# Last graph layer: one two-bank PSUM tile for a unit's turned blocks, one bank for a row's sums, one bank for the small products

## The chip, the cores and the metric

The program runs on one core of a Trainium2 chip. The metric is the device time of one execution in microseconds (us). Three executions of the kernel before gave a median of 1551.27 us (1541.69 to 1553.98).

A core has these engines: PE (matrix products and transposes, results go to PSUM only), DVE (elementwise work), ACT (activation functions), POOL, and SP, which here issues DMAs. PSUM has eight banks of 128 partitions by 512 float32 values. Both kernels use all eight in this layer.

## The reference, cut to what matters

Four graph layers run one after the other on 4096 nodes with 64 features and one 4096 x 4096 adjacency matrix. Each is followed by a residual and a layer norm. The change touches the fourth, a hyperbolic layer:

```python
deg = jnp.maximum(adj.sum(axis=1, keepdims=True), 1e-08)
w = adj / deg
log_ij = _logmap(x[:, None, :], x[None, :, :], c)
agg = jnp.einsum('ij,ijc->ic', w, log_ij)
transformed = agg @ weight + bias
return _expmap(origin, transformed, c)
```

The distance of nodes i and j is symmetric. The kernel computes a scalar factor f(i, j) for a pair once and uses it twice: times adj(i, j) for the sum of row i, and, turned, times adj(j, i) for the sum of row j.

## The kernel before, in words

The last layer starts at line 1243. Nodes are taken in 8 groups of 512. A tile is a pair of groups (i, j), with j from i on in an order `seq`, so row i of the triangle has 8, 7, ... 1 tiles, 36 in all. A tile is cut into two units of 128 x 1024 (two blocks of 128 nodes by 512), 72 in all. 28 tiles lie off the diagonal, so 56 units have a turned half.

One step of the loop at line 1508 works at several units at once, some steps apart. A unit passes through these instructions:

- `product` (L1327, PE): four instructions into a two-bank tile `v_ps`, of which there are two.
- `square` (L1336, ACT) reads `v_ps`, and `less_one` (L1353, DVE), Ln (L1520) and Exp (L1521, both ACT) follow.
- `opposite` (L1345, PE): two instructions that add to `v_ps`.
- L1545 (DVE) reads `v_ps` for the last time, which frees the tile for the product two units later. L1547 and L1556 (ACT) follow.
- L1530 (DVE) makes the factor `f`, and L1533 (DVE) multiplies the unit's piece of adj(i, j), `at_d`, by it.
- `turn` (L1371, PE): for each of the unit's two blocks of `mirrored`, four transposes of pieces of `f` into one bank of the tag `post`, and then one DVE product (L1373), 128 x 512, from that bank into `at_m`. It comes a step or two after the tile's second `f`. A tile on the diagonal turns only one half, into one bank (L1364, L1366).
- `gather` (L1387 and L1392, PE): sums over nodes. The product with `at_d` goes to the lower 64 partitions of a bank `sums_ps` and gathers through a whole row of tiles. The one with `at_m` goes to the upper 64 partitions of the same bank and lasts for one tile. A tile's upper half is added to `tb` by DVE (L1401 or L1403), and a row's lower half is copied to `tb` by ACT (L1406). A row has a `sums_ps` tile of its own.

When a row's sums are done, `finals` puts its closing steps on a list `seam`, from which each loop step takes one: `first` (L1443 on PE, then L1445 to L1448 on DVE), `second` (L1454 and L1455 on PE, L1459 on ACT, L1460 to L1462 on DVE), and three steps without PE. What is left on the list after the loop runs one after the other. At the head of the layer the list still holds closing steps of layer three (`summed` L1114, `turn_prepared` with the transposes of L212). `right` (L1283 to L1287) makes two operands for a new row through two tiles of `post`.

The order on each engine is not the order of the text. A scheduler goes through the program with an estimate of each instruction's time, gives each engine the earliest instruction of the program that it believes ready, and sets the semaphores. A tile from a pool with n buffers can be written only when the tile n allocations before it (of the same tag) has been read for the last time. Each engine then works through its list in order, and an instruction that waits holds up everything behind it on that engine.

PSUM in this layer: `ps_v3` 2 tiles of two banks, `ps_p3` 2 banks of the tag `post` (turned blocks, `right`, the diagonal's turn, `finals`, the closing steps of layer three), `ps_a3` 2 banks for `sums_ps`.

Of the kernel before, what the change touches and what calls it, by code (L numbers as in the profile page):

```python
# [9 lines left out]
F32 = mybir.dt.float32  # L10
# [4 lines left out]
ALU = mybir.AluOpType  # L15
AX = mybir.AxisListType
PSUM = bass.MemoryType.PSUM
# [43 lines left out]
def gnn4_kernel(  # L61
# [21 lines left out]
    nc = tc.nc  # L83
    P = 128
# [3 lines left out]
    GW = GB * P  # L88
# [35 lines left out]
    ident = const.tile([P, P], F32, name="ident")  # L124
# [77 lines left out]
    def cols(b):  # L202
        return slice(b * P, (b + 1) * P)
# [252 lines left out]
    with tc.tile_pool(name="acc", bufs=1) as acc_p, tc.tile_pool(name="win", bufs=1) as win_p, tc.tile_pool(  # L456
        name="cols0", bufs=4
    ) as cols_p, tc.tile_pool(name="diag0", bufs=2) as diag_p, tc.tile_pool(
        name="ps_t0", bufs=3, space=PSUM
    ) as ps_t, tc.tile_pool(name="ps_a0", bufs=1, space=PSUM) as ps_a, tc.tile_pool(  # L460
        name="ps_p0", bufs=2, space=PSUM
# [112 lines left out]
        for g in range(NG):  # L574
# [3 lines left out]
            for c in reversed(range(NCH)):  # L578
                raw = first_raw.pop() if first_raw else load_raw(g, c)
                at = (diag_p if c == g else cols_p).tile([P, CB, GW], F32, name="at", tag="at")  # L580
                for k in range(CB):
                    jb = c * CB + k
                    tp = ps_t.tile([P, GW], F32, name="tp", tag="tp")
# [466 lines left out]
    for signed in (True, False):  # L1050
        with tc.If(any_negative > 0) if signed else cmp.Else() as block:
            cmp = block
            with tc.tile_pool(name="cols1", bufs=4 if not signed else 2) as cols_p, tc.tile_pool(name="sign1", bufs=1 if signed else 5) as sg, tc.tile_pool(
                name="tail1", bufs=1
            ) as tl, tc.tile_pool(name="ps_a1", bufs=1 if signed else 2, space=PSUM) as ps_a, tc.tile_pool(
                name="ps_p1", bufs=2, space=PSUM
# [80 lines left out]
    with tc.tile_pool(name="mask2", bufs=3) as mk_p, tc.tile_pool(name="wt2", bufs=3) as wt_p, tc.tile_pool(  # L1137
        name="ps_c2", bufs=1, space=PSUM
    ) as ps_c, tc.tile_pool(name="ps_a2", bufs=1, space=PSUM) as ps_a, tc.tile_pool(
        name="ps_p2", bufs=2, space=PSUM  # L1140
# [5 lines left out]
        def gather_two(jb, half, a, wt, acc):  # L1146

            for r in range(2):
                rows = slice(r * HP, (r + 1) * HP)
                in_order(nc.tensor.matmul(  # L1150
                    acc[2 * a + r], lhsT=(sup_two if r == half else over_two)[rows, jb, :],
                    rhs=wt[half][a][rows, :].bitcast(BF16),
                    start=(jb == NB - 1 and half == 1), stop=(jb == 0 and half == 0), skip_group_check=True,
                ))
# [18 lines left out]
        gathers = []  # L1173
        busy = False
        for turn, groups in enumerate(turns_of):
            cnt = [ps_c.tile([P, GW], F32, name=f"cnt_ps{a}") for a in range(2)]
            acc = [ps_a.tile([P, GW], F32, name=f"acc_ps{q}") for q in range(QG)]
# [5 lines left out]
            for h in reversed(range(2 * NB)):  # L1183
                jb, odd = divmod(h, 2)
                c, k = divmod(jb, CB)
# [16 lines left out]
                if odd:  # L1202
                    continue
                two = [
                    lambda half=half, a=a, jb=jb, wt=wt, acc=acc: gather_two(jb, half, a, wt, acc)
                    for half in (1, 0) for a in range(2)
                ]
# [35 lines left out]
    with tc.tile_pool(name="o3", bufs=1) as op, tc.tile_pool(name="cols3", bufs=3) as cols_p, tc.tile_pool(  # L1243
        name="w3", bufs=4
    ) as wp3, tc.tile_pool(name="el3", bufs=3) as el, tc.tile_pool(name="f3", bufs=2) as fp, tc.tile_pool(
        name="r3", bufs=2
    ) as rp, tc.tile_pool(name="ps_v3", bufs=2, space=PSUM) as ps_v, tc.tile_pool(
        name="ps_p3", bufs=2, space=PSUM
    ) as ps_p, tc.tile_pool(name="ps_a3", bufs=2, space=PSUM) as ps_a:
        HB = CB // 2  # L1250

        tb = op.tile([P, N], F32, name="tb")
# [41 lines left out]
        own, mirrored = {}, {}  # L1294
# [19 lines left out]
        rights, sums, fs = {}, {}, {}  # L1314
# [40 lines left out]
        def turn(n):  # L1355

            t, h = n
            i, j = tiles[t]
            work = []
            if i == j:  # L1360
                tp = ps_p.tile([P, GW], F32, name="post", tag="post")
                for k in range(HB):
                    for b in range(HB):
                        nc.tensor.transpose(tp[:, cols(HB * k + b)], fs[t][:, b, cols(HB + k)], ident)  # L1364
                to = own[t][:, HB:CB, 0 : HB * P]
                work.append(lambda: nc.vector.tensor_tensor(to, tp.rearrange("p (k i) -> p k i", k=HB), to, ALU.mult))  # L1366
                return work
            for b in (HB * h, HB * h + 1):
                tp = ps_p.tile([P, GW], F32, name="post", tag="post")
                for k in range(CB):  # L1370
                    nc.tensor.transpose(tp[:, cols(k)], fs[t][:, k, cols(b)], ident)  # L1371
                to = mirrored[t][:, b, :]
                work.append(lambda to=to, tp=tp: nc.vector.tensor_tensor(to, tp, to, ALU.mult))  # L1373
            return work

        def gather(t, h, tm):
# [131 lines left out]
        while n < NU + 2 or turns or gathers:  # L1508
            if n % 2:
                load_own((n + 1) // 2)  # L1510
                load_mirrored((n - 1) // 2)
            after = gather(*gathers.pop(n)) if n in gathers else []
            turned = [w for what in turns.pop(n, []) for w in turn(what)]
            if n < NU:
                if n % 2 == 0:
# [8 lines left out]
            if n >= 2 and n - 2 < NU:  # L1524
                m = n - 2
                t, h = divmod(m, 2)
# [17 lines left out]
            if n < NU:  # L1544
                nc.vector.scalar_tensor_tensor(rt, vs[n][:, :, cs], V_FLOOR, rt, ALU.max, ALU.add)  # L1545
                product(n + 2)
                nc.scalar.activation(w, w, AF.Exp, bias=half_shift[:, 1:2], scale=-0.5)  # L1547
            late = turn(late_turns.pop(n)) if n in late_turns else []
            for work in after:
                work()  # L1550
# [59 lines left out]
```

## Time and profile before

| | |
|---|---|
| median of three executions | 1551.27 us (1541.69 to 1553.98) |
| the profiled execution's own time | 1546.41 us |
| its span in the trace | 1544.3 us |
| PE busy over the span | 1410.2 us (91%) |
| DVE busy over the span | 1066.9 us (69%) |
| ACT busy over the span | 761.4 us (49%) |
| first `right` of the last layer | at 1071.6 us |
| first transposes of the first off-diagonal tile | at 1103.7 us |
| `at_m` products (L1373) | 112, 75.3 us busy |
| transposes for them (L1371) | 448, 67.4 us busy |

The shares of the whole span mix four layers. The last one alone, cut near the ends of its rows (a cut is where ACT copies a row's sums, rounded), is as follows.

| stretch (us) | length | PE busy | DVE busy | ACT busy |
|---|---|---|---|---|
| 1074 to 1125 | 51 | 43.6 | 46.5 | 44.5 |
| 1125 to 1198 | 73 | 62.6 | 69.5 | 55.2 |
| 1198 to 1279 | 81 | 75.5 | 79.4 | 76.6 |
| 1279 to 1353 | 74 | 67.9 | 68.0 | 65.9 |
| 1353 to 1413 | 60 | 54.3 | 57.0 | 56.3 |
| 1413 to 1462 | 49 | 45.1 | 45.1 | 45.0 |
| 1462 to 1498 | 36 | 33.6 | 33.8 | 33.8 |
| 1498 to 1523 | 25 | 21.8 | 24.5 | 17.0 |
| 1523 to the end | 21.3 | 5.6 | 11.3 | 10.7 |

Busy time is the time in which an engine had an instruction under way, with overlaps counted once. In a line of the timeline, the first number is the start and the second the duration, both in us; what stands in brackets is the engine's idle time before it and who ended it.

### The profile page before, as it was taken

How to read it: one execution, taken by the hardware profiler on the slowest of the kernel's cores; microseconds unless marked ns; L12 is line 12 of the kernel's file. 1: busy time of each engine (PE TensorE's matmuls, PEld its weight loads, DVE VectorE, ACT ScalarE, POOL GpSimd, SP SyncE). 2: the span in 40 equal slices, each digit the busy share in tenths (PEclk: the TensorE clock that was granted, in tenths of full speed). 3: DMA queues.
4: the chain of work that ended last, by engine and by line, in shares of the span. 5: the costliest groups of instructions: out<-in, count | busy, mean ns of one | idle time of the engine just before them, and what ended most of it. 6: DMA issues, size and time to landing. Idle time of an engine off the chain costs nothing.

```text
span 1544.3 us, 19446 instructions
## 1 busy us (share of the span) xinstructions
PE 1410.2 (91%) x7054; PEld 644.7 (42%) x7054; DVE 1066.9 (69%) x2123; ACT 761.4 (49%) x1265; POOL 123.8 (8%) x194
## 2 busy tenths in 40 slices
PE   5999999999999969889899999998888999899995
PEld 4555655554443323334343333333334444344343
DVE  5899989883000663667666422556999999999997
ACT  3544434441000110222222476654877999899995
POOL 3011000000000001222222200000000000000000
PEclk9999999999999998999999999999999999999997
DMA  9999999996787987888888655553224453445430
GB/s 295 412 404 411 411 410 397 382 358 242 245 287 261 389 342 271 280 309 305 296 309 296 207 177 183 164 165 131 88 109 164 162 195 136 167 156 193 149 113 11
DMA packets 103359, 385.38 MB, mean 250 GB/s; under 512 B 16340, under 2 KB 17368, under 8 KB 71256
## 3 DMA queue, kind: packets, MB, share of 16 engines
q1 hardware_dynamic: 84256, 296.78, 53.9%
q0 software_dynamic: 15616, 85.73, 13.6%
q10 hardware_dynamic: 3384, 1.56, 0.4%
q8 instruction: 57, 0.93, 0.2%
q14 instruction: 46, 0.38, 0.1%
HBM read 297.26 MB, written 85.20 MB: 248 GB/s over the span
## 4 chain that ended last, share of the span: by engine, by line
PE 32%; DVE 18%; ACT 6%; issue 2%; DMA 2%; SPq 0%; ACTq 0%; DVEq 0%
PE v_ps L1327 5%; PE a_ps L997 4%; PE sums_ps L1387 4%; PE cnt_ps L1192 4%; PE acc_ps L1150 4%; DVE rt L1545 3%; DVE at_m L1373 3%; PE p_ps L980 2%; DVE f L1530 2%; DVE at_d L1533 2%; ACT wt L1197 2%; PE post L779 1%; DMA at<-adj_t 1%; PE p_ps L988 1%; DVE w L1353 1%
## 5 line engine op out<-in xcount | busy, mean ns | idle before, releaser
L592 ACT COPY at<-tp 128x512 f32<-128x512 f32 x256 | 132.5, 598 | 137.2 <-issue 96.0
L1327 PE MATMUL v_ps<-rv,tr_a 128*128 128x512 f32 (+1 forms) x288 | 141.5, 616 | 31.7 <-DVE rt L1545 30.3
L1197 ACT ACTIVATE wt<-cnt_ps 128x512 uint16<-128x512 f32 x208 | 115.4, 594 | 72.1 <-PE cnt_ps L1192 70.3
L585 PE MATMUL tp<-ident,raw 128*128 128x128 f32 x1024 | 133.4, 284 | 16.2 <-DMA raw<-in_adj_dram 12.0
L618 DVE TENSOR_REDUCE dpart<-raw 128x4 f32<-128x2048 f32 x64 | 145.4, 2272 | 0.4 <-DMA raw<-in_adj_dram 0.3
L620 DVE TENSOR_REDUCE lows<-raw 128x1 f32<-128x2048 f32 x64 | 145.4, 2271 | 0.0
L1387 PE MATMUL sums_ps<-at_d,nat_c 128*64 128x512 f32 x288 | 139.8, 606 | 1.4 <-DVE at_d L1533 1.0
L585 PEld LDWEIGHTS tp<-ident,raw 128*128 128x128 f32 x1024 | 116.6, 145 | 55.3 <-issue 34.1
L997 PE MATMUL a_ps<-at,nat_a 128*64 128x512 f32 x512 | 126.9, 624 | 2.9 <-DVE at L963 2.9
L447 DVE TENSOR_SCALAR pos<-at 128x2048 fp8e4<-128x2048 f32 x72 | 87.1, 1224 | 58.1 <-DMA at<-adj_t 49.3
L1392 PE MATMUL sums_ps<-at_m,nat_c 128*64 128x512 f32 x224 | 108.6, 607 | 0.0
L492 PE MATMUL w_ps<-at,cheb_n 128*128 128x512 f32 x224 | 101.1, 595 | 0.0
L492 PE MATMUL pass<-at,cheb_n 128*128 128x512 f32 x224 | 99.9, 604 | 0.7 <-DVE cheb_n L643 0.7
L1556 ACT ACTIVATE rt<-rt,one_col 128x1024 f32<-128x1024 f32 x72 | 78.7, 1095 | 22.5 <-DVE rt L1545 22.0
L1327 PEld LDWEIGHTS v_ps<-rv,tr_a 128*128 128x128 f32 x288 | 52.8, 199 | 82.7 <-DVE rt L1545 39.5
L1545 DVE SCALAR_TENSOR_TENSOR rt<-v_ps,rt 128x1024 f32<-128x1024 f32 x72 | 83.2, 1156 | 3.8 <-ACT rt L1521 3.6
L1192 PE MATMUL cnt_ps<-m,follow 128*64 128x512 fp8e4 x480 | 81.1, 391 | 4.7 <-ACT wt L1197 2.3
L1533 DVE TENSOR_TENSOR at_d<-at_d,f 128x1024 f32<-128x1024 f32 x72 | 83.2, 1156 | 0.1
L1530 DVE SCALAR_TENSOR_TENSOR f<-rt,w 128x1024 f32<-128x1024 f32 x72 | 82.9, 1158 | 0.5 <-ACT rt L1556 0.4
L1373 DVE TENSOR_TENSOR at_m<-post,at_m 128x512 f32<-128x512 f32 x112 | 75.3, 683 | 9.3 <-PE post L1371 8.6
L1336 ACT ACTIVATE w<-v_ps,one_col 128x1024 f32<-128x1024 f32 x72 | 75.7, 1053 | 11.3 <-PE v_ps L1327 10.9
L1547 ACT ACTIVATE w<-w,half_shift 128x1024 f32<-128x1024 f32 x72 | 78.7, 1094 | 0.9
(365 smaller groups left out, 2267.3 us busy)
## 6 DMA issues: line engine op xcount, KB each, us to landing
at<-adj_t SPq DMA_DIRECT2D x122, 1024.0 KB, 6.1
raw<-in_adj_dram SPq DMA_DIRECT2D x64, 1024.0 KB, 13.7
adj_t<-at POOLq DMA_DIRECT2D x64, 1024.0 KB, 8.2
at_d<-adj_t SPq DMA_DIRECT2D x36, 1024.0 KB, 4.8
at_m<-adj_t SPq DMA_DIRECT2D x28, 1024.0 KB, 6.8
mask_t<-pos POOLq DMA_DIRECT2D x64, 256.0 KB, 5.9
m<-mask_t SPq DMA_DIRECT2D x120, 128.0 KB, 2.8
m<-mask_t SPq DMA_DIRECT2D x60, 256.0 KB, 3.9
```

Of the source, the lines that this page charges most:

```text
L492: in_order(nc.tensor.matmul(ps, lhsT=cheb_n[:, jb, k : k + 2, :], rhs=rhs, start=first, stop=last))
L585: in_order(nc.tensor.transpose(tp[:, cols(b)], raw[:, b, cols(k)], ident))
L592: nc.scalar.copy(at[:, k, :], tp)
L618: in_order(nc.vector.tensor_reduce(dpart[:, g, c, :], raw, AX.X, ALU.add))
L620: in_order(nc.vector.tensor_reduce(lows[:, n : n + 1], raw.rearrange("p b j -> p (b j)"), AX.X, ALU.min))
L997: in_order(nc.tensor.matmul(ps[q * F : (q + 1) * F, :], lhsT=nat_a[:, c * CB + k, 0:F], rhs=parts[q if signed else 0][:, k, :], start=(c = ...
L1192: in_order(nc.tensor.matmul(cnt[a][r * HP : (r + 1) * HP, :], lhsT=follow, rhs=chunks[c][odd][2 * a + r][:, k, :], start=(h == 2 * NB - 1) ...
L1197: in_order(nc.scalar.activation(wt[odd][a], cnt[a], AF.Relu, scale=-128.0))
L1327: nc.tensor.matmul(vs[n][:, k, cs], lhsT=tr_a[:, cols(jb)], rhs=rights[i][0][:, cs], start=True, stop=True)
L1373: work.append(lambda to=to, tp=tp: nc.vector.tensor_tensor(to, tp, to, ALU.mult))
L1387: in_order(nc.tensor.matmul(bank[0:F, :], lhsT=nat_c[:, j * CB + k, :], rhs=own[t][:, k, :], start=(i == j and k == 0), stop=(j == seq[-1] ...
L1545: nc.vector.scalar_tensor_tensor(rt, vs[n][:, :, cs], V_FLOOR, rt, ALU.max, ALU.add)
```

## The change

`ps_p3` and `ps_a3` go from two buffers to one. A unit's eight transposes go into one tile of two banks with a tag of its own (`two`, one buffer), and one DVE product of 128 x 1024 takes the place of two of 128 x 512. All other users of `post` share one bank, and all rows share one bank for `sums_ps`. The eight banks are then 4 for `v_ps`, 1 for `post`, 2 for `two` and 1 for `sums_ps`.

```diff
-        name="ps_p3", bufs=2, space=PSUM
-    ) as ps_p, tc.tile_pool(name="ps_a3", bufs=2, space=PSUM) as ps_a:
+        name="ps_p3", bufs=1, space=PSUM
+    ) as ps_p, tc.tile_pool(name="ps_a3", bufs=1, space=PSUM) as ps_a:
...
-            for b in (HB * h, HB * h + 1):
-                tp = ps_p.tile([P, GW], F32, name="post", tag="post")
+            tp = ps_p.tile([P, HB, GW], F32, name="two")
+            for b in range(HB):
                 for k in range(CB):
-                    nc.tensor.transpose(tp[:, cols(k)], fs[t][:, k, cols(b)], ident)
-                to = mirrored[t][:, b, :]
-                work.append(lambda to=to, tp=tp: nc.vector.tensor_tensor(to, tp, to, ALU.mult))
+                    nc.tensor.transpose(tp[:, b, cols(k)], fs[t][:, k, cols(HB * h + b)], ident)
+            to = mirrored[t][:, HB * h : HB * h + HB, :]
+            work.append(lambda: nc.vector.tensor_tensor(to, tp, to, ALU.mult))
             return work
```

## The prediction

> **What bounds the kernel now.** I first read the page's shares, then the busy time by stretch, because the page mixes four layers. The stretch from the first steady steps of the last layer to its last row (columns: length, then busy us of PE, PE's weight loads, DVE, ACT, POOL):
>
> ```profile
> 1098.00:1515.00 417.00, 380.03 (x1572) 166.71 (x1570) 394.42 (x654) 374.52 (x491) 0.00 (x0) 0.99 0.40 148
> ```
>
> DVE is busy for 394.4 of 417 us (94.6%), PE for 380.0 (91%), ACT for 374.5 (90%). DVE is nearest to the bound, but PE is only 14 us behind it and ACT 20. Then the waits in nearly the same stretch (sum, times, longest, us):
>
> ```profile
> PE v_ps L1327 <- DVE rt L1545: 24.2, 31, 2.6
> ACT rt L1556 <- DVE rt L1545: 22.0, 25, 2.5
> DVE at_m L1373 <- PE post L1371: 8.6, 11, 2.2
> PE post L1371 <- DVE at_m L1373: 6.4, 13, 1.3
> ```
>
> PE and ACT mostly wait for DVE (24.2 and 22.0), which agrees with DVE as the bound. The last two rows are the subject of the change: DVE stood for turned blocks, and PE for a free `post` bank. One unit on DVE, from the timeline:
>
> ```profile
> 1256.79 0.69 DVE L1353 TENSOR_SCALAR w<-w 128x1024 f32<-128x1024 f32 x1
> 1257.40 1.22 DVE L1530 SCALAR_TENSOR_TENSOR f<-rt,w 128x1024 f32<-128x1024 f32 x1
> 1258.65 0.69 DVE L1373 TENSOR_TENSOR at_m<-post,at_m 128x512 f32<-128x512 f32 x1
> 1259.26 1.22 DVE L1533 TENSOR_TENSOR at_d<-at_d,f 128x1024 f32<-128x1024 f32 x1
> 1260.53 0.69 DVE L1373 TENSOR_TENSOR at_m<-post,at_m 128x512 f32<-128x512 f32 x1
> 1261.14 1.22 DVE L1545 SCALAR_TENSOR_TENSOR rt<-v_ps,rt 128x1024 f32<-128x1024 f32 x1
> 1262.27 0.68 DVE L1353 TENSOR_SCALAR w<-w 128x1024 f32<-128x1024 f32 x1
> ```
>
> The next starts come before the recorded ends: a 512-wide product is followed after 0.61 us (recorded 0.69), a 1024-wide one after 1.13 (1261.14 to 1262.27; recorded 1.22). The unit takes 5.48 us on DVE. The durations by shape:
>
> ```profile
> L1545 DVE SCALAR_TENSOR_TENSOR rt<-v_ps,rt 128x1024 f32<-128x1024 f32 x64 | 77.8, 1216 | 3.8 <-ACT rt L1521 3.6
> L1373 DVE TENSOR_TENSOR at_m<-post,at_m 128x512 f32<-128x512 f32 x112 | 75.3, 683 | 9.3 <-PE post L1371 8.6
> ```
>
> L1545 reads a two-bank PSUM tile and a tensor in SBUF, as the new product will, so 1216 ns is the new product's price.
>
> **What the Trainium skill says.** "Perfetto Trace Analysis", section Optimizing Scalar/DVE Operations, puts DVE's access overhead per instruction at about 125 ns on PSUM, half of what is recorded overlapping with the next instruction; it adds that larger operations help a saturated engine. The trace gives 2 x 683 - 1216 = 150 ns by recorded durations and 2 x 0.61 - 1.13 = 0.09 us by starts: the same order, on both sides of the page's figure. The same page, section Identifying Performance Opportunities, says that a repeated gap on the engine that should be saturated can mean too few PSUM buffers; here that is 8.6 us of DVE in 417. "PSUM — Partial Sum Buffer", section PSUM bank collisions raise a hardware error, asks for guards by bank, so a DVE read of a bank and the next PE write to it must take turns; the 6.4 us above are such turns.
>
> **The change part by part.**
>
> *One product for two.* 56 units lose one DVE instruction each: 56 x 0.09 = 5.0 us by starts, 56 x 0.150 = 8.4 by records. I take 0.11 each, 6.2 us, and of that nine tenths, since DVE is busy 94.6% and PE and ACT have little more room: -5.5 (ends 0 and -8.4).
>
> *The transposes' bank.* Count on PE is unchanged (448). A unit's eight now wait for the one product of the unit before. In the unit above the product would stand where the first `at_m` does, 1258.65 to about 1259.8, and PE reaches its transposes at 1260.3 to 1260.8, behind the sums and L1345. Half a microsecond or more is left, and PE idles 0.47 us before the next L1327 at 1262.41 anyway. That cover hides it; without the cover it costs PE whatever the product is late. Before, the second bank came free only at 1261.2, so half of the 6.4 us of PE waits should go. PE is not the bound: 0.
>
> *Less company in `post`.* The turned blocks no longer share banks with `right`, `finals` and the diagonal's turn. Near 1300 to 1307 both banks were held by `right`, whose copies ACT made at 1302.26 and 1302.83, and DVE then waited 1.74 us for transposes. I let six tenths of the 8.6 us go, -5, and charge the other waits for eight transposes in place of four: eight take 1.09 us at 1306.78, so 0.5 more for about 3 of them, +1.5. Sum about -3.5 (ends -8.6, all gone, and +6, eleven waits each 0.55 longer).
>
> *One bank for sums.* A new row's first sums now wait for ACT's copy of the old row. At the second row's end:
>
> ```profile
> 1278.16 0.69 DVE L1403 TENSOR_TENSOR tb<-sums_ps,tb 64x512 f32<-64x512 f32 x1
> 1278.18 1.98 PE L1327 MATMUL v_ps<-rv,tr_a 128*128 128x512 f32 x4
> 1279.22 0.56 ACT L1406 COPY tb<-sums_ps 64x512 f32<-64x512 f32 x1
> ...
> 1280.09 0.64 PE L1387 MATMUL sums_ps<-at_d,nat_c 128*64 128x512 f32 x1
> ```
>
> The copy ends at 1279.78, 0.31 us ahead of the next sums; at the other six row ends it is 0.32 to 1.15. Product L1327 on PE hides it. Behind the waiting sums stand L1345 and the transposes, and for those wait L1545 and `at_m`. Price 0; without that cover at most one ACT instruction (1.1 us) at 7 row ends, +8.
>
> *One bank for small products.* Inside the rows, `right`'s second product waits for ACT's copy of the first (about 0.6 us, 8 times), and at a row's start L1443 waits for L1366, which came at 1204.23, two microseconds after L1443 began at 1202.23. PE idled 1.13 us before 1204.37 and 0.47 on other steps, so most is covered; I put +1 (ends 0 and +7).
>
> *The tail.* Here nothing covers it. The last two rows close one after the other:
>
> ```profile
> 1519.19 1.08 PE L1443 MATMUL post<-spread,tb 128*128 128x65 f32 x8 [0.44 <-DVE th L1482]
> ...
> 1523.12 0.16 DVE L1447 SCALAR_TENSOR_TENSOR al<-al,post 128x4 f32<-128x4 f32 x1
> ...
> 1523.89 1.06 PE L1443 MATMUL post<-spread,tb 128*128 128x65 f32 x8
> ...
> 1525.23 0.41 DVE L1460 TENSOR_TENSOR agg<-post,al 128x256 f32<-128x256 f32 x1
> ...
> 1525.70 0.69 PE L1454 MATMUL post<-spread_w,tb 128*128 128x64 f32 x2 [0.75 <-DVE agg L1460]
> ```
>
> With two banks, row 7's `second` began at 1522.06 beside its `first`, which DVE read until 1523.28, and row 8's `first` ran while `second` held the other bank. With one, row 7's `second` begins 1.2 us later, and behind its L1460 row 8's `first` comes whole: 1.06 on PE, then L1445 to L1447 (1526.67 to 1527.74 before, 1.07), and only then L1454. Sum 1.2 + 1.06 + 1.07 and a few handovers: 3.3 to 4.5, taken as +4.
>
> *Sum:* -5.5 - 3.5 + 0 + 1 + 4 = -4, against the profiled execution's span of 1544.3 and its own 1546.41, that is 1540.3 and 1542.4. That execution lies 4.86 under the median shown; I put the same 4 on the median: 1551.27 - 4 = 1547.3. What is late next in the stage is PE, whose own instructions come to about 5.4 us a unit (1267.61 to 1272.98 without a wait, 5.37).
>
> **The rivals.**
>
> *The shared banks were the real loss* (0.12). If all 8.6 us of DVE's waits go, the DVE saving is whole (8.4) and the smaller waits around them shrink by a further 7 of the 22.6 us in which DVE idled, the stage gains 24 and the tail returns 4: 1531. For it: the stretch 1279 to 1353, with 6 us idle on DVE, has such waits. Against: PE has 37 us of room in 417 and ACT 42, in small pieces.
>
> *DVE time saved is not time saved* (0.25). From 1413 to 1462 PE, DVE and ACT are busy 45.1, 45.1 and 45.0 of 49 us. If the three take turns as the limit everywhere, the stage gives 1 or 2 us and the tail costs 4: 1554.
>
> *The other side, slower* (0.08): the single `two` tile makes PE wait. Place: between L1345 and L1327. It decides when the product ends later than about 1261 in the unit above, that is, when the scheduler puts it behind L1545. It then ends 1262.27 + 1.13 = 1263.4, and the transposes start 2.6 us late, 2.1 beyond the idle 0.47. In one unit of four that is 14 x 2.1 = +29, with the -4 about 1576. For it: the product cannot start until all eight transposes are there, so it falls back in the order more easily. Against: L1545 stands later in the program than the product, and the margins above.
>
> That the merged product costs twice as much across two banks is excluded by L1545's 1216 ns.
>
> **How the numbers follow.** Forecast 0.55 (1541 to 1553, its own range: the ends of its terms partly cancel), rivals 0.12, 0.25 and 0.08. About 1% is what a measurement of this kernel can tell from no change: faster is under 1535.8, slower above 1566.8. The first rival lies under that, the last above it, the rest between: 0.12, 0.80, 0.08. For 8 in 10 the range takes the forecast and the null case, plus the part of the first rival that falls short of its full size: 1536 to 1558.
>
> **What would show it.** Right: 56 `at_m` products of about 1216 ns; DVE busy in the stretch some 5 to 8 us less; DVE's wait on L1371 below 5 us; PE's waits on `at_m` not above 6; L1406 ended before the next L1387; the time from the last sums to the end about 4 longer. Wrong: PE waits on `at_m` of tens of us, `at_m` behind L1545 on DVE, sums that wait for L1406, or a stage shortened by more than 15.

## The result and the profile after

The kernel after takes 1556.4 us (median of 11, 1549.16 to 1559.62), the kernel before 1548.62 (median of 11 measured beside it, 1541.69 to 1553.98). The ratio is 1.0052, with a 95% interval of 1.0034 to 1.0071: slower by some 8 us. The number lies inside the predicted range, but the predicted sign was wrong.

The profiled execution of after took 1558.9 us. Its page begins:

```profile
span 1557.1 us, 19410 instructions
...
PE 1418.1 (91%) x7054; PEld 649.7 (42%) x7054; DVE 1064.8 (68%) x2067; ACT 759.8 (49%) x1265; POOL 123.9 (8%) x194
```

PE is busy for 8 us more than before, DVE for 2 less. The first row below is the stretch of the prediction; the second runs from the layer's first L1327 to the last row's copy L1406, which I call the body; the third is a piece of the layer's start. The columns are those of the prediction; the last three numbers are PE's granted clock, the DMA share and GB/s:

```profile
1098.00:1515.00 417.00, 380.94 (x1563) 166.66 (x1563) 390.08 (x597) 374.73 (x479) 0.00 (x0) 0.98 0.40 148
1080.19:1530.42 450.23, 407.95 (x1649) 179.00 (x1648) 419.65 (x685) 392.24 (x515) 0.00 (x0) 0.97 0.39 143
1075.00:1085.00 10.00, 8.35 (x16) 3.80 (x16) 6.24 (x38) 2.76 (x7) 0.00 (x0) 0.50 1.01 423
```

The same body in the kernel before:

```profile
1074.16:1522.91 448.75, 404.40 (x1656) 178.04 (x1656) 423.58 (x745) 394.05 (x517) 0.00 (x0) 0.98 0.39 147
```

A fixed stretch of time holds another piece of the work when a layer begins later, so I compare bodies. DVE is busy for 3.9 us less, and yet the body is 1.5 us longer. The 12.8 us between the two spans split into four (layer three's sums end with the copies L1215):

| part (us) | before | after | difference |
|---|---|---|---|
| up to the first copy L1215 of layer three's last sums (unchanged code) | 1067.23 | 1069.87 | +2.64 |
| from there to the first L1327 | 6.93 | 10.32 | +3.39 |
| body | 448.75 | 450.23 | +1.48 |
| tail: last row's copy L1406 to the end | 21.39 | 26.68 | +5.29 |

The first part is this one execution's own. The second is its own by half. The layer's start, first before, then after:

```profile
1069.77 2.00 PE L1114 MATMUL post<-wd,sums 128*128 128x64 f32 x16 [2.36 <-DVE sums L1215]
1071.61 1.84 PE L1283 MATMUL post<-tr_a,to_right 128*66 128x512 f32 x2
1073.37 0.58 PE L1286 MATMUL post<-sp_two,to_other 128*2 128x512 bf16 x1
```

```profile
1072.41 3.68 PE L1114 MATMUL post<-wd,sums 128*128 128x64 f32 x16 [2.36 <-DVE sums L1215]
1077.02 1.94 PE L1283 MATMUL post<-tr_a,to_right 128*66 128x512 f32 x2 [0.94 <-DVE ln_st L275]
1079.68 0.58 PE L1286 MATMUL post<-sp_two,to_other 128*2 128x512 bf16 x1 [0.71 <-ACT rv L1284]
```

The sixteen L1114 took 3.68 us in after and 2.00 before. PE's granted clock was 0.50 from 1072 to 1077 in after, and 1.00 before, from 1069.7 to 1071.7. These 1.7 us are not the change's: number 2, whose code is that of before here, has them too. The other 1.7 us are the change's. With one small bank, `right`'s first product stands 0.94 us, until DVE has read the bank of L1114 (L1120, ended at 1076.88; the trace names the instruction behind it), and its second 0.71, until ACT has copied the first. Six of the kernels below with one small bank and L1114 at 2.00 us (numbers 1, 3, 5, 6, 10 and 12) take 8.65 us from L1215 to the first L1327; the three with two or three banks and the same L1114 (before, numbers 4 and 11) take 6.75 to 6.93. Start (+1.7), body and tail together give +8.5, which is close to the +7.8 between the medians. Some of the waits from 1100 to 1515 in after (sum, times, longest, us):

```profile
ACT w L1336 <- PE v_ps L1327: 15.0, 20, 2.1
PE v_ps L1327 <- DVE rt L1545: 14.5, 21, 2.7
PE two L1371 <- DVE at_m L1373: 9.2, 11, 1.5
DVE w L1353 <- ACT w L1336: 6.1, 7, 1.6
DVE agg L1460 <- ACT v L1459: 4.6, 5, 1.7
DVE at_m L1373 <- PE two L1371: 4.5, 8, 1.1
```

DVE's own wait for turned blocks has fallen from 8.6 to 4.5 and PE's wait for `rt` from 24.2 to 14.5. But PE now waits longer for the turned tile (6.4 to 9.2), ACT waits longer for the product (6.8 to 15.0), and DVE waits for ACT's square (0.8 to 6.1). At five row ends DVE also stands before L1460 of `second`, for ACT's L1459 (0.2 to 4.6). The groups by shape show the new product at the price taken for it:

```profile
L1545 DVE SCALAR_TENSOR_TENSOR rt<-v_ps,rt 128x1024 f32<-128x1024 f32 x64 | 78.0, 1219 | 4.3 <-ACT rt L1521 3.0 <-PE v_ps L1345 1.1
L1373 DVE TENSOR_TENSOR at_m<-two,at_m 128x1024 f32<-128x1024 f32 x56 | 68.3, 1220 | 5.5 <-PE two L1371 5.0
```

The timeline of after at a place where two turned units follow one another, and in the tail:

```profile
1343.50 0.98 PE L1371 MATMUL two<-ident,f 128*128 128x128 f32 x7
...
1344.53 1.23 DVE L1373 TENSOR_TENSOR at_m<-two,at_m 128x1024 f32<-128x1024 f32 x1 [0.50 <-PE two L1371]
1345.66 1.22 DVE L1545 SCALAR_TENSOR_TENSOR rt<-v_ps,rt 128x1024 f32<-128x1024 f32 x1
...
1345.80 1.09 PE L1371 MATMUL two<-ident,f 128*128 128x128 f32 x8 [1.10 <-DVE at_m L1373]
...
1522.37 0.64 PE L1387 MATMUL sums_ps<-at_d,nat_c 128*64 128x512 f32 x1 [1.18 <-ACT tb L1406]
...
1526.69 1.10 PE L1443 MATMUL post<-spread,tb 128*128 128x65 f32 x8
...
1530.63 0.16 DVE L1447 SCALAR_TENSOR_TENSOR al<-al,post 128x4 f32<-128x4 f32 x1
...
1530.93 0.41 PE L1454 MATMUL post<-spread_w,tb 128*128 128x64 f32 x2 [1.28 <-DVE ln_ve L246]
...
1533.90 0.43 DVE L1460 TENSOR_TENSOR agg<-post,al 128x256 f32<-128x256 f32 x1 [1.34 <-ACT v L1459]
1534.38 1.97 PE L1443 MATMUL post<-spread,tb 128*128 128x65 f32 x8 [1.48 <-DVE agg L1460]
...
1537.60 0.66 PE L1454 MATMUL post<-spread_w,tb 128*128 128x64 f32 x2 [1.25 <-DVE nv L1470]
```

Two things are to be seen. At 1344 the one tile makes turns strict: transposes, product, transposes. The second eight cannot start before the product ends at 1345.76, and PE stands for 1.10 us although the factors were there. In the tail the four steps stand in one chain through the one bank: row 7's `first` at 1526.69, its `second` only after L1447, row 8's `first` only after L1460, and row 8's `second` only after that row's L1447.

### The profile page after: what moved, and what is told of

It reads as the page before. It is cut to its first block, busy times and chain, and to the rows that moved or that the text cites. A ratio compares the mean times of both kernels' runs of the same rounds, so it can differ in the third digit from the quotient of the medians.

```text
span 1557.1 us, 19410 instructions
## 1 busy us (share of the span) xinstructions
PE 1418.1 (91%) x7054; PEld 649.7 (42%) x7054; DVE 1064.8 (68%) x2067; ACT 759.8 (49%) x1265; POOL 123.9 (8%) x194
## 4 chain that ended last, share of the span: by engine, by line
PE 63%; DVE 19%; ACT 6%; issue 6%; DMA 4%; ACTq 1%; SPq 1%; POOL 1%; DVEq 0%; POOLq 0%
PE tp L585 7%; PE pass L492 6%; PE w_ps L492 6%; PE v_ps L1327 5%; PE a_ps L997 4%; PE sums_ps L1387 4%; PE cnt_ps L1192 4%; PE acc_ps L1150 4%; PE pass L485 3%; PE h_ps L485 3%; DVE rt L1545 3%; DVE at_m L1373 2%; PE post L506 2%; PE p_ps L980 2%; DVE f L1530 2%
## 5 line engine op out<-in xcount | busy, mean ns | idle before, releaser
L1327 PE MATMUL v_ps<-rv,tr_a 128*128 128x512 f32 (+1 forms) x288 | 144.0, 624 | 18.8 <-DVE rt L1545 18.3
L997 PE MATMUL a_ps<-at,nat_a 128*64 128x512 f32 x512 | 123.7, 611 | 2.9 <-DVE at L963 2.9
L1556 ACT ACTIVATE rt<-rt,one_col 128x1024 f32<-128x1024 f32 x72 | 78.7, 1095 | 18.6 <-DVE rt L1545 18.1
L1545 DVE SCALAR_TENSOR_TENSOR rt<-v_ps,rt 128x1024 f32<-128x1024 f32 x72 | 83.4, 1159 | 4.3 <-ACT rt L1521 3.0
L1327 PEld LDWEIGHTS v_ps<-rv,tr_a 128*128 128x128 f32 x288 | 53.2, 202 | 76.9 <-issue 41.9
L1521 ACT ACTIVATE rt<-w,half_shift 128x1024 f32<-128x1024 f32 x72 | 78.5, 1094 | 0.6
```

What stands on the lines that cost most here:

```text
L997: in_order(nc.tensor.matmul(ps[q * F : (q + 1) * F, :], lhsT=nat_a[:, c * CB + k, 0:F], rhs=parts[q if signed else 0][:, k, :], start=(c = ...
L1327: nc.tensor.matmul(vs[n][:, k, cs], lhsT=tr_a[:, cols(jb)], rhs=rights[i][0][:, cs], start=True, stop=True)
```

## The experiments

The theories at the start: the tail is the loss, and the rows gain nothing because what DVE saves comes back as waits for the one tile; or the rows lose because `right`, `finals` and the diagonal's turn take turns in one small bank; or the single sums bank costs. The banks are those of after unless an edit says otherwise. "Rows" are the times between copies L1406 (seven intervals).

**1. The tail alone.** The last two rows' `second` writes to the turned tile, idle by then.

```diff
-                o = ps_p.tile([P, GB, 2, F], F32, name="post", tag="post")
+                if g in seq[-2:]:
+                    o = ps_p.tile([P, HB, GW], F32, name="two")[:, 0, :].rearrange("p (b t f) -> p b t f", b=GB, t=2)
+                else:
+                    o = ps_p.tile([P, GB, 2, F], F32, name="post", tag="post")
```

> The changed kernel, with one difference: the second step of the last two rows takes its PSUM from the turned blocks' two-bank tile, which has no other use by then. Theory (the one small bank makes the two last rows close in single file): the stretch from the last copy of sums to the end falls from 26.7 us back to 21 to 22.5, and the time falls by 4 to 5.5 us, to 1551 to 1552.5. Rival (the loss is in the rows, the longer tail is an effect of the clock there): the stretch stays at 25 to 27 and the time at 1555 to 1557.

1551.83 us, ratio to before 1.0015 (1.0002 to 1.0028), 4.6 less than after. Its tail in the timeline (L1457 is the old L1454):

```profile
1524.82 1.11 PE L1443 MATMUL post<-spread,tb 128*128 128x65 f32 x8
...
1527.71 0.43 PE L1457 MATMUL two<-spread_w,tb 128*128 128x64 f32 x2
...
1528.76 0.16 DVE L1447 SCALAR_TENSOR_TENSOR al<-al,post 128x4 f32<-128x4 f32 x1
...
1531.18 1.45 PE L1443 MATMUL post<-spread,tb 128*128 128x65 f32 x8 [1.47 <-ACT tb L1406]
...
1532.42 0.63 PE L1457 MATMUL two<-spread_w,tb 128*128 128x64 f32 x2
```

Row 7's `second` now runs ahead of its L1447, and row 8's two steps stand close together. The tail falls from 26.68 to 20.15. Rows stay as in after (326.81 against 324.78; six of the seven agree within 0.02 us, the last is 2.0 longer because the last copy now comes later). So the tail's part of the loss is shown.

**2. One bank for sums alone**, in the kernel before.

```diff
-    ) as ps_p, tc.tile_pool(name="ps_a3", bufs=2, space=PSUM) as ps_a:
+    ) as ps_p, tc.tile_pool(name="ps_a3", bufs=1, space=PSUM) as ps_a:
```

> The kernel before with one bank for the rows' sums and nothing else changed (one PSUM bank stays unused). Theory (the copy of a row's sums is hidden): 1548 to 1550, at most one of seven row ends with a wait of a microsecond. Rival (one bank for the sums is what costs): 1552 to 1556, with waits of the first sums of a row for the copy at several row ends.

1549.2 us, ratio 0.9997 (0.9982 to 1.0013). The rows take 324.36 us, against 324.35. The bank costs nothing.

**3. The new division of the banks without the merged product:** two products of 128 x 512, each block in a bank of its own (`ps_t` is a pool of two banks).

```diff
-            tp = ps_p.tile([P, HB, GW], F32, name="two")
-            for b in range(HB):
+            for b in (HB * h, HB * h + 1):
+                tp = ps_t.tile([P, GW], F32, name="two")
...
-            to = mirrored[t][:, HB * h : HB * h + HB, :]
-            work.append(lambda: nc.vector.tensor_tensor(to, tp, to, ALU.mult))
+                to = mirrored[t][:, b, :]
+                work.append(lambda to=to, tp=tp: nc.vector.tensor_tensor(to, tp, to, ALU.mult))
```

> The changed kernel's banks (one for small products, one for sums, two for turned blocks alone) with the old two products of 128x512 per unit. It tells the merging from the banks. Theory (the merged product gains about 5 us in the rows, the banks lose): slower than the changed kernel, 1558 to 1563. Rival (the merged product with its single two-bank tile holds the rows up): faster than the changed kernel, 1549 to 1554.

1558.94 us, ratio 1.0068 (1.0051 to 1.0085). The body takes 448.92 us, between before (448.75) and after (450.23), and the tail 29.61. As the tails differ by 2.9 us from after's, this pair does not price the merging cleanly; number 12 does. DVE's wait for turned blocks falls from 8.6 to 4.2 us, but at five row ends DVE stands 1.6 us each before L1462 (the old L1460), 7.9 in all, against 0.2 before.

**4. Shared banks:** the kernel before with the freed sums bank given to `post`.

```diff
-        name="ps_p3", bufs=2, space=PSUM
-    ) as ps_p, tc.tile_pool(name="ps_a3", bufs=2, space=PSUM) as ps_a:
+        name="ps_p3", bufs=3, space=PSUM
+    ) as ps_p, tc.tile_pool(name="ps_a3", bufs=1, space=PSUM) as ps_a:
```

> The kernel before with one bank for sums and three shared banks for all transposes and small products, two products per unit. Theory (sharing banks with the small products cost DVE waits; a third bank removes them, and the tail keeps two banks): 1543 to 1547. Rival (DVE, PE and ACT take turns as the limit, so fewer waits for banks give nothing): 1547 to 1551.

1540.67 us, ratio 0.9929 (0.9899 to 0.9958): faster than both kernels. Body and waits from its profile:

```profile
1079.15:1523.17 444.02, 402.80 (x1640) 178.89 (x1664) 422.58 (x748) 392.87 (x521) 0.00 (x0) 0.98 0.40 149
```

```profile
PE v_ps L1327 <- DVE rt L1545: 20.4, 25, 2.6
...
DVE at_m L1373 <- PE post L1371: 4.5, 5, 1.8
...
PE post L1371 <- DVE at_m L1373: 3.3, 7, 1.1
```

DVE is as busy as before (422.6 against 423.6), with all 112 products, but DVE's and PE's waits for each other over turned blocks fall together: 8.6 to 4.5 and 6.4 to 3.3. DVE's wait before L1460 is 1.4. The body is 4.7 us shorter. The tail, 19.33, is 2.1 shorter than before; row 8's `first` and `second` find free banks one behind the other:

```profile
1523.80 1.10 PE L1443 MATMUL post<-spread,tb 128*128 128x65 f32 x8 [1.47 <-ACT tb L1406]
1524.74 0.39 PE L1454 MATMUL post<-spread_w,tb 128*128 128x64 f32 x2
```

Numbers 3 and 4 have the same eight banks and the same instructions and stand 18 us apart; they differ in whether three banks are shared or tied to uses (2 + 1). Of that, 15.2 lie behind the first L1327 (10.3 in the tail and 4.9 in the body, but the last row is 3.2 us shorter in number 3, which moves the cut between the two) and 1.8 at the layer's start.

**5. `right` made later**, four steps ahead and not six, on top of number 1. If `right` in the one small bank holds up the rows, it should then meet `finals` less.

```diff
-            if n + 6 < NU and tiles[(n + 6) // 2][0] not in rights:
-                i = tiles[(n + 6) // 2][0]
+            if n + 4 < NU and tiles[(n + 4) // 2][0] not in rights:
+                i = tiles[(n + 4) // 2][0]
```

> The changed kernel with the tail's second step in the two-bank tile, and the operands of a new row made four loop steps ahead in place of six, after the old row's second step has left the small bank. Theory (in the rows the small products stand in each other's way in their one bank): the rows that the changed kernel made longer, the fourth (62.0 us) and the sixth (39.5), come back to 59 to 60 and 35 to 37, and the time falls from 1551.8 to 1545 to 1549. Rival (those rows are long because the merged product makes the order on the engines worse, not because of the small bank): rows four and six stay within 1 us of 62.0 and 39.5, the time at 1550 to 1553.

1557.41 us, ratio 1.0061 (1.0037 to 1.0085), so 5.6 slower than number 1. The sixth row came back from 39.54 to 36.13, but the second, fourth and fifth grew (80.00 to 85.05, 61.99 to 63.45, 46.55 to 51.35). The theory of `right` explains one row and not the sum. It is not refuted either: number 8 shows that the later `right` costs 4.4 us where three banks are shared, so this edit can bring a loss of its own; but numbers 12 and 6, where the same step costs nothing (1551.66 and 1549.15), have one small bank too.

**6. Two products, tail freed, lead of four:** number 3 with the same tail edit (`second` of the last two rows from `ps_t`) and the edit of number 5.

> As the one before, but with two products of 128x512 per unit from two banks of their own: the two kernels differ in the merging alone. Theory (merging saves DVE time, but DVE, PE and ACT take turns as the limit, so little of it is saved time): within 3 us of the kernel with the merged product. Rival (merging saves what DVE saves, 4 to 8 us, once the small bank is out of the way): 4 to 8 us slower than it.

1549.15 us, ratio 1.0004 (0.9992 to 1.0017). With the later `right` the merged form (number 5) is 8.3 us slower than the two products.

**7. `second` of all rows in the turned tile:** the edit of number 1 without its condition.

> The changed kernel with the second step of all rows, not of the last two alone, in the turned blocks' tile: one kind of small product moves from the small bank to the other one. Theory (a bank tied to one use waits while the other is free; sharing is what the old kernel had right): rows four and six shorter than 62.0 and 39.5 by 1 to 3 us each, time 1547 to 1551. Rival (turned blocks then wait for the second step, which ACT and DVE read late): rows 1 to 3 us longer, time 1553 to 1560.

1552.55 us, ratio 1.0025 (1.0012 to 1.0038). Rows four and six shrink against number 1 (61.99 to 58.13, 39.54 to 37.74), row two grows (80.00 to 87.28); the sum is 1.0 longer. Freeing the small bank everywhere gains nothing either: DVE no longer stands before L1460 (4.6 us in number 1), but it waits longer for the sums (L1403, 1.3 to 6.3 us).

**8. Number 4 with the lead of four.**

> Control for the lead of four steps: the kernel with three shared banks and one bank for sums, with the operands of a row made four steps ahead. Theory (the lead matters only where the small bank is single): within 2 us of 1540.7. Rival (the shorter lead is better or worse by itself): differs by over 3 us.

1545.1 us, ratio 0.9965 (0.995 to 0.998), 4.4 slower than number 4 (the intervals overlap slightly); rows 324.17 against 319.55. A change of two steps in the program's text moves the rows by as much as the banks do.

**9. Merged product with shared tiles:** number 1 with the turned blocks and the last `second` steps in a third tile of `v_ps`.

```diff
-    ) as rp, tc.tile_pool(name="ps_v3", bufs=2, space=PSUM) as ps_v, tc.tile_pool(
+    ) as rp, tc.tile_pool(name="ps_v3", bufs=3, space=PSUM) as ps_v, tc.tile_pool(
...
-            tp = ps_p.tile([P, HB, GW], F32, name="two")
+            tp = ps_v.tile([P, HB, GW], F32, name="two", tag="v_ps")
```

> Merged products whose two-bank tile is not tied to the turned blocks: three two-bank tiles shared by v_ps and the turned blocks, one bank for small products, one for sums, the tail's second step in a shared tile. Theory (banks tied to one use are what the merged product loses by): rows shorter than the 324.8 us of the changed kernel by 4 to 8, time 1544 to 1549. Rival (the turned blocks take tiles from the products of v_ps, which PE then cannot start in time): rows longer by 5 to 20, time 1556 to 1572.

1550.64 us, ratio 1.0019 (0.9998 to 1.004). PE's wait moves to the distance product:

```profile
PE v_ps L1327 <- DVE at_m L1373: 32.0, 29, 2.8
```

Tiles of one tag go round in order, so L1327 gets the tile that the last merged product still reads. Sharing is not good by itself; here it ties the main product to the turned one.

**10. Two products from the one two-bank tile.** All else is as in after.

```diff
-            to = mirrored[t][:, HB * h : HB * h + HB, :]
-            work.append(lambda: nc.vector.tensor_tensor(to, tp, to, ALU.mult))
+            for b in range(HB):
+                to = mirrored[t][:, HB * h + b, :]
+                work.append(lambda b=b, to=to: nc.vector.tensor_tensor(to, tp[:, b, :], to, ALU.mult))
```

> The changed kernel with two products of 128x512 read out of the one two-bank tile, so that the first need not wait for all eight transposes, while both banks still come free together. Theory (little of DVE's time is saved time, and the tile held as one costs PE): rows within 3 us of the changed kernel's 324.8, time 1554 to 1560. Rival (the wait for all eight transposes is what eats the gain): rows 4 us or more shorter, time 1549 to 1552.

1563.06 us, ratio 1.0081 (1.0049 to 1.0112), 6.7 slower than after, with intervals that overlap. The traces give 6.0 for body and tail, but 4.5 of it is the tail, where neither kernel has a turned product; the body is 1.5 longer, and the rows are level (324.23 against 324.78). So that merging is right with the one tile is not shown. `PE two <- DVE at_m` is 13.2 us here: two smaller products do not shorten PE's wait as long as the tile is one.

**11. What a microsecond of DVE is worth:** before with one of a unit's two mirrored products left out.

```diff
-                work.append(lambda to=to, tp=tp: nc.vector.tensor_tensor(to, tp, to, ALU.mult))
+                if b == HB * h:
+                    work.append(lambda to=to, tp=tp: nc.vector.tensor_tensor(to, tp, to, ALU.mult))
```

> The kernel before with one of a unit's two products of a turned block left out (the transposes stay), so the sums of mirrored blocks are not the reference's. It takes 56 products of 0.61 us by starts, 34 us of DVE time, away and measures how much of DVE's time is time of the kernel. Theory (DVE, PE and ACT take turns as the limit): 8 to 18 us faster, a quarter to a half of 34. Rival (DVE is the bound, as the prediction took it, nine tenths): 27 to 34 us faster.

1526.07 us, ratio 0.984 (0.9802 to 0.9878), 22.5 less than before. Its body:

```profile
1076.31:1506.47 430.16, 400.73 (x1664) 179.01 (x1664) 394.00 (x693) 391.53 (x518) 0.00 (x0) 0.98 0.41 154
```

DVE's busy time falls by 29.6 us in the body and the body by 18.6: 0.63 of it. On the medians, 22.5 of 29.6 is 0.76, with an interval (18.9 to 30.7 us) that does not exclude nine tenths. DVE is the main bound, but with PE at 400.7 and ACT at 391.5 of 430 us over a third of what it saves in the body is lost. The edit also frees one of a unit's two banks without a read, so the 0.63 is not the worth of DVE's time alone.

**12. The pair of number 1 without the merging:** number 3 with the tail edit only.

> Two products of 128x512 from two banks of their own and the tail's second step in one of these, with the old lead of six steps: it differs from the changed kernel with the mended tail (1551.83) in the merging alone, the third such pair. Theory (the merging's effect has no steady sign; the order the scheduler lays down decides): the tail 19 to 21, the time 1546 to 1554. Rival (merging saves the DVE time that it takes away, two thirds of 4 to 8 us): 1554.5 to 1557. Rival (merging loses, as with the lead of four): below 1547.

1551.66 us, ratio 1.0017 (1.0001 to 1.0033), against 1551.83 for number 1. The two differ in the merging alone (one product and one tile for two), and no difference shows; the intervals are 2 to 2.5 us to either side. In the traces body and tail together are 470.5 us here and 472.3 in number 1. Some of the waits from 1100 to 1515, first of number 12 (lines shifted by two), then of number 1:

```profile
PE v_ps L1329 <- DVE rt L1550: 16.6, 25, 2.1
...
ACT w L1338 <- PE v_ps L1329: 9.8, 12, 1.9
...
DVE agg L1465 <- ACT v L1464: 7.9, 5, 1.6
...
DVE at_m L1375 <- PE two L1373: 4.2, 5, 1.5
...
PE two L1373 <- DVE at_m L1375: 1.7, 6, 0.3
```

```profile
ACT w L1336 <- PE v_ps L1327: 15.3, 19, 2.2
...
PE v_ps L1327 <- DVE rt L1548: 13.6, 20, 2.9
PE two L1371 <- DVE at_m L1373: 11.6, 11, 2.2
DVE w L1353 <- ACT w L1336: 7.1, 7, 1.6
...
DVE agg L1463 <- ACT v L1462: 4.6, 5, 1.7
DVE at_m L1373 <- PE two L1371: 4.5, 8, 1.1
```

With the same two banks, the merged form makes PE wait 11.6 us for the turned tile in place of 1.7. ACT waits 5.5 more for the distance product, and DVE 5.1 more for ACT's square (7.1 against 2.0). In number 12 DVE's largest wait in these rows is that before L1465 (the old L1460): `second` begins late, its last part runs behind a distance product (L1329, 1373.59 to 1375.53 at the third row's end), and DVE stands 1.57 us.

## Why the prediction was wrong, point by point

**One product for two: -5.5 predicted. The failed step, together with the next.** The new product costs what was said (1220 ns), and there are 56. But DVE's busy time from the first L1327 to the end falls only from 434.97 to 432.23, by 2.7 us; in the two pairs that differ in the merging it falls by 2.2 (number 3 to after) and 1.9 (number 12 to number 1). So the 0.11 us a unit, 6.2 in all, was too much: 0.03 to 0.05 is measured. (The 125 ns of the Trainium skill, "Perfetto Trace Analysis", section Optimizing Scalar/DVE Operations, is the engine's busy time, so it stands beside the 0.09 by starts; the page has about twice that for recorded durations, and the 150 ns belong beside that.) The figures were read where DVE runs without a gap. An instruction that has waited has nothing to overlap with, and DVE waits 34 times from 1100 to 1515 in after against 29 before; at some 0.09 each that is half a microsecond, so why DVE saves no more is not shown in full. At the 0.63 to 0.76 of number 11, in place of nine tenths, 2.7 us would be worth about 2.

**The transposes' bank: 0 predicted ("Half a microsecond or more is left", "PE is not the bound: 0").** This is the step that took the saving back. It looked at one unit whose transposes came late enough. Where two turned units follow one another, nothing is left: 1.10 us at 1345.80, eleven such waits, 9.2 us where at most 6 had been named. The words about half of the 6.4 going away were right for two banks of the turned blocks' own (1.7 us, number 12) and wrong for one tile over both. The predicted rival of a slower kernel had the right mechanism but the wrong place and size: it asked for a product behind L1545, with 2.1 us in one unit of four, and the runs show waits of about 0.8 us in a fifth of the units. Pair 12 and 1 puts the two failed steps together: what merging saves on DVE, the single tile takes back, with a net near 0 where -5.5 had been forecast (and a loss of 8.3 in the pair 5 and 6).

**Less company in `post`: -3.5 predicted.** The wait did fall as said, from 8.6 to 4.5. But with own banks and two products (number 3) the body is 448.92 us against 448.75, so nothing of the 3.5 is left. What the sum had missed is `second` in the one small bank: DVE's waits for turned blocks fell by 4.4 us, and those before L1460 rose by 7.7. In number 4 the first wait falls nearly as far, the second stays at 1.4, and the body is 4.7 us shorter.

**One bank for sums: 0.** Right, by number 2. In after, PE waits for the copy near the end (1.18 us at 1522.37) and number 1 has the same.

**One bank for small products: +1.** Too small, and this step failed as well. At the layer's start alone it costs 1.7 us, shown above; the prediction had named `right`'s second product there, but neither its first nor a price for the start. In the rows the prediction wrote out the chain from `first` to `second` for the tail only, and in the one small bank DVE then stands 4.6 us (after) to 7.9 (numbers 3 and 12) before L1460. What these waits cost in time is not separated: number 7 removes them and its rows are no shorter. The first row is about 1 us longer with one small bank (125.1 to 125.5 us in after and numbers 1, 3 and 12; 124.1 to 124.5 in before and numbers 2 and 4), which agrees, but the later rows change with the order of the instructions too.

**The tail: +4.** Right in mechanism and a little small: 5.3. The chain is the one that was written down. What is missing is PE's pace: row 8's L1443 takes 1.97 us and not 1.06, which is 0.9 of the 1.3 us that the estimate was short. PE's granted clock was 0.50 there, from 1534 to 1537, and 1.00 before, from 1523 to 1525. The gap of 1.48 us ahead of it does not explain the pace by itself: in number 4 the same instructions took 1.10 behind a gap of 1.47, at a clock of 1.00.

**Sum.** Start and body -8 predicted, +3.2 measured (+1.7 and +1.5); tail +4 predicted, +5.3 measured. With the tail mended, number 1 is still 2.7 us behind before (0.3 to 4.3), of which the start is 1.7. In the null rival ("the stage gives 1 or 2 us and the tail costs 4") the size was nearest, but its reason, that DVE time saved is not time saved, is only partly so: number 11 shows that it mostly is. That the number fell inside the range is luck: the range was drawn to hold this rival too, and the forecast's own sum had the wrong sign.

**What stays open.** Single rows change by 1 to 5 us between kernels with the same banks (number 1 and 5, number 4 and 8), with the order that the scheduler lays down. Rows with the same order repeat to some 0.03 us, so these are real differences, but no run says what in the order makes them. So why numbers 5 and 6 stand 8.3 us apart, where 1 and 12 stand level, and how much of number 4's 4.7 us in the body is its third shared bank, are not settled. PE's granted clock over the body is 0.97 in all kernels with the merged product (after, 1, 5, 7 and 9) and 0.98 in all others; no run tells whether this lower clock is an effect of PE's waits or adds to the merged form's loss. The 18 us between numbers 3 and 4 are measured; that sharing explains the start's and the tail's part is shown by the timeline, the body's part is argued from the waits.

## What to carry to other kernels

Joining two evacuations (reads that empty a PSUM tile) into one saved 0.03 to 0.05 us of DVE each here, and it makes one buffer of two: look for the place where the same producer comes twice in a row, and price the wait there, not in a unit picked from the middle. The Trainium skill has a rule near this one in "Perfetto Trace Analysis", section Optimizing Scalar/DVE Operations: where DVE is not saturated but makes bubbles on other engines, smaller instructions may let work end sooner. This case agrees only in part: PE waits 1.7 us with two products from two tiles and 11.6 with one from one (numbers 12 and 1), but 13.2 with two products from one tile (number 10), so here it is the second tile that shortens the wait. When a bank is taken from small products, ask in every row, and not only at the end, which engine stands when they come late. When a bank comes free, try it first in the pool that most users share (1540.67 us here, number 4) before tying banks to uses (1558.94, number 3), and follow a kernel's last steps by hand, since nothing covers them.

## What was not expected of the hardware

- The same eight L1443 took 1.06 to 1.11 us in the lines above at a granted clock of 1.00, and 1.97 in after's tail at 0.50. The gap ahead does not tell the two apart: 1.10 us behind a gap of 1.47 (number 4), 1.45 behind 1.47 (number 1, clock 0.70 from 1531 to 1533), 1.97 behind 1.48 (after).
- At the layer's start PE's granted clock was 0.50 from 1072 to 1085 in after, and an L1114 instruction took 0.23 us there in place of 0.13. The kernels' starts (first L1215 to first L1327) spread from 6.75 us (number 11) to 10.32 (after). Number 2, whose code there is that of before, has 8.65 against 6.93, with L1114 at 3.67 us; so up to 2 us of a start is the execution's own.
